# A four-layer graph network in one kernel: softmax and RMS factors laid along the free axis by block transposes instead of by bf16 products

## The chip, the cores and the metric

The kernel runs on one core of a Trainium2 chip. Its time is the device time in microseconds from start to end of one execution. A core has engines that run side by side and meet at semaphores: TensorE (PE, matrix products into PSUM), VectorE (DVE), ScalarE (ACT), GpSimd (POOL) and the queue of SyncE (SP), which issues the transfers between device memory and the on-chip memory SBUF. Each engine works through its own instructions strictly in their order. SBUF and PSUM have 128 partitions; data runs along the free axis inside each of them.

## The reference

There are 32 graphs of 512 nodes, with 256 features each and a 512x512 adjacency matrix. Four layers follow each other, each inside a residual sum and a layer norm:

```python
x = LN(x + attention(x, adj))         # 8 heads of 32, masked by adj
x = LN(x + W2 relu(W1 ((1+eps) x + adj x)))
h = W1 (eps x + adj x) + b1           # 1024 wide
x = LN(x + W2 silu(h * rsqrt(mean(h^2) + 1e-6) * w) + b2)
x = LN(x + softplus(xn W_self + (xn - s_out adj s_in xn) W_neigh))
```

Two factors concern us. The softmax divides each head's output by the sum of its exponentials, one number per node and head. The RMS norm of the third layer multiplies all 1024 hidden values of a node by one number. Everything is computed in float32.

## The kernel before

Hidden values are kept transposed: features on partitions, the 512 nodes along the free axis (oT for the attention's output, gT for the third layer's hidden values). The two factors, however, come out with nodes on partitions, 128 nodes in each of NT = 4 tiles, so they have to be laid along the free axis and repeated over the partitions before they can multiply oT or gT.

For this, `split` (L917) cuts a factor into three bf16 parts whose sum is the float32 number (L924, L931). The parts are transposed on TensorE (pm_t, L941) and copied to SBUF (mT). Products with constant selector matrices then add the three parts and repeat them over partitions: `spread` (pr_r, L970) for the softmax, once per graph for both groups of four heads, and `spread_rms` (pb, L1321) for the RMS. `normalise` (L953) does so after both calls of `attend`: the reciprocals of all 32 sums (L959), the split, pr_r, and the products with oT (L981). oT itself has been copied from PSUM by `evacuate` before. For the RMS, squares of gT are added into ssq by POOL (L554), ssq is block-transposed (L1277) and reduced (L1280), a small product pm (L1288) adds over partitions, two DVE operations pick each node's own number (L1302, L1310), POOL raises it to -0.5 (L572), then come split and pb, and eight DVE operations scale gT (L1333). Silu (L1348) and the w22 product (L998) follow.

In `attend` (L770) the scores sc use row quadrants of TensorE (32 rows each, four heads side by side), and the weighted sums po_att (L900) use column quadrants. Transposing the exponentials takes a DVE block transpose (L858) and a round trip through device memory (L870, L882); graph 0 uses TensorE for it.

The order of all work is not that of the code. Each operation is recorded with its engine, an assumed cost, and what it reads and writes. The class `Order` lays out one graph to find due times, adds a constant per stage (`LEAD`), and gives graph b the key b times `PERIOD` plus that. A list planner then places the operations of all graphs; among those that can start soon the smallest key wins, with penalties for changing TensorE's tiling (`TURN_DUE`) and ACT's table. So several graphs are interleaved, and every engine's queue is fixed before the run. Tiles come from rings of buffers: four PSUM banks for most products, one set of four banks for sc.

Of the kernel before, what the change touches and what calls it, by code (L numbers as in the profile page):

```python
# [9 lines left out]
F32 = mybir.dt.float32  # L10
# [6 lines left out]
P = 128  # L17
# [2 lines left out]
RMS_EPS = 1e-6  # L20
HEADS = 8

PERIOD = 68064
LEAD = {
    "adjT": 136800, "agg1": -11000, "agg2": -29700, "degree": 92400, "diag": 77700,
    "lap": -82300, "ln0": -24200, "ln1": -117600, "ln2": -21700, "ln3": 9700, "load": -153500,
    "move": 42300, "pv": 19300, "pz": 26900, "qk": 7500, "rinv": -106100, "rms": -114100,
    "scores": -6200, "silu": 94000, "softplus": -156100, "v": -89600, "w11": -216800,
    "w12": -58400, "w21": 15900, "w22": -12100, "wo": 64800, "x3T": 800, "xT": 6200,
}  # L30


# [27 lines left out]
class Order:  # L60
# [9 lines left out]
    TABLE, TABLE_DUE = 1300, 9000  # L70

    TURN = {"whole": 93, "row": 290, "col": 150}
    TURN_DUE = 750
    LATE = 0.13
    HASTE = 90

    def __init__(self):
        self.ops = []
# [209 lines left out]
def kernel(  # L288
# [48 lines left out]
    make_identity(nc, ident)  # L337
    ones = const.tile([P, P], F32, name="ones")
    nc.vector.memset(ones, 1.0)
    nhalf = const.tile([P, NT], F32, name="nhalf")  # L340
    nc.vector.memset(nhalf, -0.5)

    ident_b = const.tile([P, P], BF16, name="ident_b")
    nc.vector.tensor_copy(ident_b, ident)

    def selector(n, wide, name):

        of = const.tile([P, n], F32, name=f"{name}_of")
        nc.vector.tensor_reduce(
            of, ident[:, 0 : 3 * n].rearrange("p (r x) -> p x r", r=3), axis=AX.X, op=ALU.add
        )
        sel = const.tile([P, n, wide], BF16, name=name)
        nc.vector.tensor_copy(sel, of.unsqueeze(2).to_broadcast([P, n, wide]))
        return sel

    NX = 2 * NT * HPG
    sel_r = selector(NX, HD, "sel_r")  # L360
    sel_t = selector(NT, P, "sel_t")


    id_as = ident.rearrange("p (a s) -> p a s", a=4)
# [3 lines left out]
    nc.vector.tensor_copy(quad, place.unsqueeze(1).to_broadcast([P, 4, 32]))  # L368
    own = const.tile([P, 4], F32, name="own")
    nc.vector.tensor_reduce(own, id_as, axis=AX.X, op=ALU.add)  # L370
    nc.vector.tensor_single_scalar(own, own, 1.0 / F2, op=ALU.mult)

    order = Order()

# [138 lines left out]
    def graph(b):  # L513
# [10 lines left out]
        def tmp(shape, tag, bufs, name=None, dtype=F32):  # L524
            return Buf(sb, shape, dtype, tag, f"{name or tag}_{b}", bufs)

        def pe(cost, fn, r, w, *hold, turn="whole"):

            op([("PE", cost, fn, {"turn": turn})], r, w, hold)

        def dve(cost, fn, r, w, port=False):
            op([("DVE", cost, fn, {"port": 1} if port else {})], r, w)
# [4 lines left out]
        def pool(cost, fn, r, w):  # L537
            op([("POOL", cost, fn, {})], r, w)
# [4 lines left out]
        def evacuate(dst, src, r, w):  # L543
            either(
                r, w,
                (690, lambda: nc.vector.tensor_copy(dst(), src())),
                (590, lambda: nc.scalar.copy(dst(), src())),
            )
# [19 lines left out]
                port=True,  # L568
            )

        def rsqrt(dst, src, r, w):
            pool(1020, lambda: nc.gpsimd.tensor_tensor(dst(), src(), nhalf, ALU.pow), r, w)  # L572

        def small(name, bufs=2, shape=None):
            return Buf(sb, shape or [P, NT], F32, "s_" + name, f"{name}_{b}", bufs)
# [194 lines left out]
        def attend(g):  # L770
# [5 lines left out]
            for t in range(NT):  # L776
# [113 lines left out]

                if t < NT - 1:
                    continue
                stage[0] = "pv"

                def pv():

# [10 lines left out]

                pe(
                    3500, pv,
                    [(pT, a) for pT in pTs for a in range(4)] + [(v, c) for c in range(NT)],  # L910
                    [(po,)], oT, turn="col",
                )

            stage[0] = "rinv"
            evacuate(lambda: oT[:, g, :], po, [(po,)], [(oT, g)])

        def split(src, n, name):  # L917

            parts = tmp([P, 3, n], "p_" + name, 2, name + "p", dtype=BF16)
            left, left_k = src, []  # L920
            for r in range(3):
                dve(
                    190,
                    lambda r=r, left=left: nc.vector.tensor_copy(parts[:, r, :], left()),  # L924
                    [(left,)], [(parts, r)], port=True,
                )
                if r < 2:
                    rest = small(name + "rest", 2, [P, n])
                    dve(
                        180,  # L930
                        lambda r=r, left=left, rest=rest: nc.vector.tensor_tensor(  # L931
                            rest(), left(), parts[:, r, :], ALU.subtract
                        ),
                        [(left,), (parts, r)], [(rest,)], port=True,
                    )
                    left = rest
            pm_t = Buf(ps, [P, P], BF16, "m", f"pm_t_{b}", 4)
            mT = tmp([P, P], "mT_" + name, 1, dtype=BF16)
            pe(
                65,  # L940
                lambda: nc.tensor.transpose(  # L941
                    pm_t[0 : 3 * n, :], parts().rearrange("p r x -> p (r x)"), ident_b
                ),
                [(parts, r) for r in range(3)], [(pm_t,)], mT,
            )
            either(
                [(pm_t,)], [(mT,)],
                (220, lambda: nc.vector.tensor_copy(mT[0 : 3 * n], pm_t[0 : 3 * n, :])),
                (330, lambda: nc.scalar.copy(mT[0 : 3 * n], pm_t[0 : 3 * n, :])),
            )  # L950
            return mT

        def normalise():  # L953

            stage[0] = "rinv"
            rv = small("rv", 2, [P, NX])
            dve(
                240,
                lambda: nc.vector.reciprocal(rv(), rs().rearrange("p g t j -> p (g t j)")),  # L959
                [(rs, g, t, j) for g in range(2) for t in range(NT) for j in range(HPG)],  # L960
                [(rv,)],
            )
            mT = split(rv, NX, "sums")
            for g in range(2):
                pr_r = bank("pr_r")

                def spread(g=g, pr_r=pr_r):
                    for t in range(NT):
                        x = (g * NT + t) * HPG
                        nc.tensor.matmul(  # L970
                            pr_r[:, t * P : (t + 1) * P],
                            lhsT=sel_r[0 : 3 * NX, x : x + HPG].rearrange("p j e -> p (j e)"),
                            rhs=mT[0 : 3 * NX],
                            start=True,
                            stop=True,
                        )

                pe(240, spread, [(mT,)], [(pr_r,)])
                dve(
                    700,  # L980
                    lambda g=g, pr_r=pr_r: nc.vector.tensor_tensor(  # L981
                        oT[:, g, :], pr_r(), oT[:, g, :], ALU.mult
                    ),
                    [(pr_r,)], [(oT, g)],
                )

        def pair_sum(lhs, lhs_k, w, w_k, nk, y, step):

# [101 lines left out]
        values()  # L1090
        attend(0)
        attend(1)
        normalise()
        stage[0] = "wo"
        pair_sum(oT, lambda k: (oT, k), wo, "wo", DC, y, DC)

# [198 lines left out]
            [(red,)], [(pm,)],  # L1295
        )

        mine = small("mine", 1, [P, NT, 4])
        ms = small("ms")

        def mean_square():
            nc.vector.scalar_tensor_tensor(  # L1302
                out=mine(),
                in0=pm[:, 0 : 4 * NT].rearrange("p (t i) -> p t i", i=4),
                scalar=RMS_EPS * F2,
                in1=own.unsqueeze(1).to_broadcast([P, NT, 4]),
                op0=ALU.add,
                op1=ALU.mult,
            )
            nc.vector.tensor_reduce(ms(), mine(), axis=AX.X, op=ALU.add)  # L1310

        dve(400, mean_square, [(pm,)], [(ms,), (mine,)])
        rr = small("rr")
        rsqrt(rr, ms, [(ms,)], [(rr,)])

        mT = split(rr, NT, "rms")
        pb = bank("pb")

        def spread_rms():
            for t in range(NT):  # L1320
                nc.tensor.matmul(  # L1321
                    pb[:, t * P : (t + 1) * P],
                    lhsT=sel_t[0 : 3 * NT, t],
                    rhs=mT[0 : 3 * NT],
                    start=True,
                    stop=True,
                )

        pe(240, spread_rms, [(mT,)], [(pb,)])
        for m in range(C2):  # L1330
            dve(
                750,
                lambda m=m: nc.vector.scalar_tensor_tensor(  # L1333
                    out=gT[:, m, :],
                    in0=gT[:, m, :],
                    scalar=rw_c[:, m : m + 1],
                    in1=pb(),
                    op0=ALU.mult,
                    op1=ALU.mult,
                ),  # L1340
                [(pb,), ("rw_c",)], [(gT, m)],
            )
        stage[0] = "silu"
        for hf in range(2):
# [256 lines left out]
```

## Time and profile before

| | us |
|---|---|
| median of three runs (lowest, highest) | 3340.49 (3338.41, 3343.99) |
| the profiled execution | 3344.47 |
| its span, first to last instruction | 3342.7 |
| TensorE busy | 3290.4 |
| VectorE busy | 2672.3 |
| ScalarE busy | 1957.1 |
| GpSimd busy | 841.5 |

Busy time is the time in which an engine has at least one instruction running. A float32 product shows as two records, and the records' ends overlap those that follow, so the time a group of products takes is read from its start to the next group's start. The granted TensorE clock was 0.995 of full.

### The profile page before, as it was taken

Reading aid. Unit: us, or ns where it says so; the run is one execution under the profiler, and the core shown is the slowest. Engines: PE = TensorE matmul, PEld = TensorE weight load, DVE = VectorE, ACT = ScalarE, POOL = GpSimd, SP = SyncE. Lnnn points to the kernel's source line nnn. Section 1 sums busy time; section 2 is a strip of 40 time slices with the busy share of each in tenths; the row PEclk is TensorE's granted clock in tenths of the full one; section 3 lists DMA queues with packets and bytes.
Section 4 is the critical chain, followed back from the end, with each engine's and each line's share of the span. In section 5 each row is a group of like instructions: output and inputs, shape, how many; then the busy total and the mean of one; then the engine's idle time right before and its main releaser. Section 6 shows DMA issues by size and latency. Waiting matters only on the chain.

```text
span 3342.7 us, 54840 instructions
## 1 busy us (share of the span) xinstructions
PE 3290.4 (98%) x19624; PEld 1983.0 (59%) x19624; DVE 2672.3 (80%) x6191; ACT 1957.1 (59%) x4056; POOL 841.5 (25%) x611
## 2 busy tenths in 40 slices
PE   8999999999999999999999999999999999999997
PEld 5456665566665566655566655666555666556654
DVE  8878887788887888887888877888878888778855
ACT  6456656556665656665655656566656566656533
POOL 1222222222222222222222222222222222222221
PEclk9999999999999999999999999999999999999999
DMA  6788777777777777887777877877877877877710
GB/s 155 234 230 233 197 207 224 199 226 209 206 216 224 201 218 208 211 225 203 216 215 198 218 224 196 225 206 205 225 215 201 222 205 204 234 196 210 199 38 26
DMA packets 768193, 677.21 MB, mean 203 GB/s; under 512 B 540208, under 2 KB 592304, under 8 KB 736176
## 3 DMA queue, kind: packets, MB, share of 16 engines
q1 hardware_dynamic: 767920, 673.71, 73.7%
q8 instruction: 155, 2.54, 0.3%
q14 instruction: 118, 0.97, 0.1%
HBM read 380.52 MB, written 293.08 MB: 202 GB/s over the span
## 4 chain that ended last, share of the span: by engine, by line
PE 93%; DVE 2%; ACT 2%; DMA 1%; SPq 1%; issue 0%; POOL 0%; POOLq 0%; DVEq 0%; ACTq 0%
PE po L998 23%; PE ph L1177 13%; PE pg L1194 13%; PE sc L784 8%; PE po_att L900 7%; PE pa L1194 7%; PE pq L711 6%; PE pa_l L1485 6%; PE pz L1443 6%; PE pv L752 3%; SPq L595 1%; ACT pq L822 1%; DVE pq L858 0%; PE pr_r L970 0%; DMA xnT<-x3d 0%
## 5 line engine op out<-in xcount | busy, mean ns | idle before, releaser
L822 ACT ACTIVATE pq<-pq,mx 128x512 f32<-128x512 f32 x1024 | 729.1, 713 | 311.6 <-DVE mx L808 292.1
L808 DVE CUSTOM_DVE_ANT_0 pq<-sc,bias 128x512 f32<-128x512 f32 x1024 | 664.7, 683 | 96.5 <-PE sc L784 88.9
L858 DVE STREAM_TRANSPOSE pq<-pq 128x2048 f32<-128x2048 f32 x248 | 569.9, 2298 | 152.6 <-ACT pq L822 151.8
L1194 PE MATMUL pg<-hT,w 128*128 128x512 f32 x1024 | 470.1, 599 | 0.3 <-DVE zy L1454 0.2
L998 PE MATMUL po<-w,gT 128*128 128x256 f32 x2048 | 450.1, 380 | 6.8 <-ACT gT L1348 6.8
L998 PEld LDWEIGHTS po<-w,gT 128*128 128x128 f32 x2048 | 389.8, 191 | 64.4 <-ACT gT L1348 9.6
L554 POOL TENSOR_TENSOR ssq<-ssq,sq 128x512 f32<-128x512 f32 x218 | 277.4, 1272 | 593.2 <-ACT sq L1270 593.2
L1051 POOL TENSOR_TENSOR rstd<-ve,nhalf 128x4 f32<-128x4 f32 (+1 forms) x132 | 134.4, 1018 | 846.4 <-DVE ve L1046 845.4
L1194 PEld LDWEIGHTS pg<-hT,w 128*128 128x128 f32 x1024 | 189.2, 190 | 261.9 <-issue 219.9
L784 PE MATMUL sc<-kT,qT 32*128 32x512 f32 x2048 | 292.9, 641 | 0.0
L900 PEld LDWEIGHTS po_att<-pT,v 128*32 128x32 f32 x8192 | 219.9, 110 | 51.6 <-DVE zy L1454 21.2
L1443 PE MATMUL pz<-wsn,xnT 128*128 128x512 f32 x512 | 242.0, 599 | 3.9 <-DVE s_in L1118 2.2
L900 PE MATMUL po_att<-pT,v 128*32 128x128 f32 x8192 | 237.8, 274 | 3.9 <-DMA pT<-via 3.9
L1177 PE MATMUL ph<-adjT,y_att 128*128 128x512 f32 x512 | 230.5, 603 | 0.0
L998 PE MATMUL po<-w,aT 128*128 128x256 f32 x1024 | 229.5, 382 | 0.0
L1485 PE MATMUL pa_l<-zy,adjT 128*128 128x256 f32 x1024 | 229.2, 382 | 0.0
L1194 PE MATMUL pa<-hT,w 128*128 128x512 f32 x512 | 228.3, 599 | 0.0
L1177 PE MATMUL ph<-adjT,y 128*128 128x512 f32 x512 | 227.5, 596 | 0.0
L998 PEld LDWEIGHTS po<-w,aT 128*128 128x128 f32 x1024 | 192.0, 190 | 48.4 <-issue 22.0
L1485 PEld LDWEIGHTS pa_l<-zy,adjT 128*128 128x128 f32 x1024 | 192.1, 190 | 26.4 <-issue 0.9
L1270 ACT ACTIVATE sq<-gT 128x512 f32<-128x512 f32 x224 | 140.1, 625 | 92.2 <-POOL ssq L554 45.8
L822 ACT ACTIVATION_READ_ACCUMULATOR pq<-pq,mx 128x1 f32 x1024 | 192.2, 188 | 0.0
(166 smaller groups left out, 4687.0 us busy)
## 6 DMA issues: line engine op xcount, KB each, us to landing
via<-pq SPq DMA_DIRECT2D x992, 256.0 KB, 5.1
pT<-via SPq DMA_DIRECT2D x248, 1024.0 KB, 6.7
adj<-in_adj_dram SPq DMA_DIRECT2D x32, 1024.0 KB, 8.6
adjT<-in_adj_dram SPq DMA_DIRECT2D x124, 256.0 KB, 7.1
y_att<-in_x_dram SPq DMA_DIRECT2D x32, 512.0 KB, 4.2
xT<-in_x_dram SPq DMA_DIRECT2D x124, 128.0 KB, 4.0
x3d<-y SPq DMA_DIRECT2D x31, 512.0 KB, 2.9
xnT<-x3d SPq DMA_DIRECT2D x124, 128.0 KB, 7.3
```

Of the source, the lines that this page charges most:

```text
L554: lambda: nc.gpsimd.tensor_tensor(dst(), dst(), src(), ALU.add), {},
L711: nc.tensor.matmul(pq(), lhsT=w[:, c, m * P : (m + 1) * P], rhs=xT[:, c, :], start=(c == 0), stop=(c == DC - 1),)
L784: nc.tensor.matmul(sc[:, j, :], lhsT=qT[hp, g, t * P : (t + 1) * P], rhs=kTs[g][hp, :], start=True, stop=True,)
L808: lambda t=t, j=j, sc=sc, row=row: nc.vector.tensor_tensor_reduce(out=row(), in0=sc[:, j, :].rearrange("p (a n) -> p a n", a=4), in1=bias[ ...
L822: lambda t=t, j=j, row=row: nc.scalar.activation(row(), row(), AF.Exp, bias=mx[:, t, j : j + 1], scale=-1.0, accum_out=rs[:, g, t, j : j + 1],
L858: lambda pq=pq: nc.vector.transpose(pq().rearrange("p a j c s -> p (a j c s)"), pq().rearrange("p a j c s -> p (a j c s)"),),
L900: nc.tensor.matmul(po[j * HD : (j + 1) * HD, t * P : (t + 1) * P], lhsT=v[:, c, h * HD : (h + 1) * HD], rhs=pTs[t][:, :, j, c, :], start=( ...
L998: nc.tensor.matmul(po[:, i * D : (i + 1) * D], lhsT=lhs[:, k, t * P : (t + 1) * P], rhs=w[:, k, :], start=(i == 0 and k == 0), stop=(i == ...
L1177: nc.tensor.matmul(ph(), lhsT=xin[:, m, c * P : (c + 1) * P], rhs=adjT[:, m, :], start=(m == 0), stop=(m == NT - 1),)
L1194: nc.tensor.matmul(pa(), lhsT=w[:, c, m * P : (m + 1) * P], rhs=hT[:, c, :], start=(c == 0), stop=(c == DC - 1),)
L1443: nc.tensor.matmul(pz(), lhsT=xnT[:, c, t * P : (t + 1) * P], rhs=wsn[:, c, :], start=(c == 0), stop=(c == DC - 1),)
L1485: nc.tensor.matmul(pa[:, i * D : (i + 1) * D], lhsT=adjT[:, m, t * P : (t + 1) * P], rhs=zy[:, m, D : 2 * D], start=(m == 0), stop=(m == N ...
```

## The change

The selectors, `split`, `normalise`, pm_t, pr_r and pb are gone. A new helper `along` does the laying out: a DVE transpose in blocks of 32x32 whose source is a column repeated 32 times, so that one instruction gives a 128x512 tile.

For the softmax, each call of `attend` now takes the reciprocals of its own 16 sums, multiplies them with the constant own (a mask that keeps, on each partition, one of four quarters) into parts, and a small product pf, per head, in column quadrants with 16 columns, spreads them; `along` makes fac from pf. po_att is recorded as waiting for pf. Its result is multiplied with fac straight from PSUM, with no copy before.

For the RMS, the two picking operations become one on all 16 columns, POOL's power takes 16 columns, and `along` makes the tile that scales gT. The scale 1/F2 moves from own into that operation.

The planner's parameters are other ones too, so the whole order changes. The number of products on TensorE falls from 10116 to 9924. Per graph: two pm_t, eight pr_r and four pb go, eight pf come.

```diff
-PERIOD = 68064
+PERIOD = 73093
 LEAD = {
...
-    TURN_DUE = 750
-    LATE = 0.13
-    HASTE = 90
+    TURN_DUE = 2500
+    LATE = 0.00
+    HASTE = -18005
...
-    nhalf = const.tile([P, NT], F32, name="nhalf")
+    nhalf = const.tile([P, 4 * NT], F32, name="nhalf")
...
+        def along(dst, src, r, w):
+            dve(
+                700,
+                lambda: nc.vector.transpose(
+                    dst().rearrange("p (x r) -> p x r", r=32),
+                    src().unsqueeze(2).to_broadcast([P, 4 * NT, 32]),
+                ),
+                r, w,
+            )
...
+                    160, lambda: nc.vector.reciprocal(rv(), rs[:, g]),
...
+                    lambda: nc.vector.tensor_tensor(
+                        parts().rearrange("p j t i -> p (j t) i"),
+                        rv().rearrange("p t j -> p j t").unsqueeze(3).to_broadcast([P, HPG, NT, 4]),
+                        own.unsqueeze(1).to_broadcast([P, HPG * NT, 4]),
+                        ALU.mult,
+                    ),
...
+                def quadrants():
+                    for j in range(HPG):
+                        nc.tensor.matmul(
+                            pf[j * HD : (j + 1) * HD, 0 : 4 * NT],
+                            lhsT=quad[:, 0, :],
+                            rhs=parts[:, j].rearrange("p t i -> p (t i)"),
+                            start=True,
+                            stop=True,
+                        )
+                pe(
+                    120, quadrants,
+                    [(parts,)] + [(pT, a) for pT in pTs for a in range(4)]
+                    + [(v, c) for c in range(NT)],
+                    [(pf,)], fac, turn="col",
+                )
+                along(fac, lambda: pf[:, 0 : 4 * NT], [(pf,)], [(fac,)])
...
-            evacuate(lambda: oT[:, g, :], po, [(po,)], [(oT, g)])
...
+                lambda: nc.vector.tensor_tensor(oT[:, g, :], po(), fac(), ALU.mult),
+                [(po,), (fac,)], [(oT, g)],
...
-        normalise()
...
+        ms, rr = (small(n, 1, [P, 4 * NT]) for n in ("ms", "rr"))
+        dve(
+            170,
+            lambda: nc.vector.tensor_scalar(
+                ms(), pm[:, 0 : 4 * NT], scalar1=1.0 / F2, scalar2=RMS_EPS,
+                op0=ALU.mult, op1=ALU.add,
+            ),
+            [(pm,)], [(ms,)],
+        )
+        rsqrt(rr, ms, [(ms,)], [(rr,)], 4 * NT)
+        along(ssq, rr, [(rr,)], [(ssq,)])
```

## The prediction

> **What bounds the kernel now.** I read the page first: busy times and slices.
>
> ```profile
> PE 3290.4 (98%) x19624; PEld 1983.0 (59%) x19624; DVE 2672.3 (80%) x6191; ACT 1957.1 (59%) x4056; POOL 841.5 (25%) x611
> ...
> PE   8999999999999999999999999999999999999997
> ```
>
> TensorE is busy for 98% of the span; only the first and last slices fall short. The windows say where the other 2% lies (columns: window, length, busy us of PE, weight loads, DVE, ACT, POOL, then clock and DMA).
>
> ```profile
> 1500.00:1600.00 100.00, 100.00 (x602) 59.73 (x602) 81.12 (x187) 59.45 (x127) 26.40 (x19) 1.00 0.75 214
> ...
> 0.00:300.00 300.00, 279.77 (x1941) 169.45 (x1942) 245.85 (x578) 174.12 (x397) 60.30 (x48) 0.99 0.76 209
> 3100.00:3342.00 242.00, 210.97 (x1094) 136.02 (x1092) 149.36 (x366) 98.70 (x156) 49.69 (x40) 0.95 0.34 86
> ```
>
> Idle at the head are 20 us, at the tail 31; of the 51 to 52 in all (3342.7 - 3290.4) nothing is left for the middle. So a graph costs what its TensorE instructions take, and the next view is TensorE's timeline over one period (start, length, tile). Two equal softmax products (po_att) start at 1513.73 and 1615.38 us: a period of 101.65 us, 32 of them in the span.
>
> ```profile
> 1544.17 1.14 PE L784 MATMUL sc<-kT,qT 32*128 32x512 f32 x8
> 1545.24 0.26 PE L941 MATMUL pm_t<-ident_b,sumsp 128*96 128x128 bf16 x1
> 1545.34 1.94 PE L711 MATMUL pq<-xT,wk 128*128 128x512 f32 x4
> 1547.11 0.61 PE L970 MATMUL pr_r<-mT_sums,sel_r 96*128 96x128 bf16 x8
> 1547.56 7.08 PE L1177 MATMUL ph<-adjT,y 128*128 128x512 f32 x16
> ...
> 1577.71 1.14 PE L784 MATMUL sc<-kT,qT 32*128 32x512 f32 x8
> 1578.78 3.70 PE L900 MATMUL po_att<-pT,v 128*32 128x128 f32 x128
> 1582.41 0.40 PE L1288 MATMUL pm<-red,quad 128*128 128x16 f32 x2
> 1582.65 7.15 PE L1485 MATMUL pa_l<-zy,adjT 128*128 128x256 f32 x32
> 1589.64 1.03 PE L752 MATMUL pv<-wv,xT 128*128 128x256 f32 x4
> 1590.60 0.22 PE L941 MATMUL pm_t<-ident_b,rmsp 128*12 128x128 bf16 x1
> 1590.75 1.99 PE L752 MATMUL pv<-wv,xT 128*128 128x256 f32 x8
> 1592.68 0.39 PE L1321 MATMUL pb<-mT_rms,sel_t 12*128 12x128 bf16 x4
> 1593.00 1.13 PE L752 MATMUL pv<-wv,xT 128*128 128x256 f32 x4
> ```
>
> Ends overlap, so I cost everything from start to next start.
>
> **TensorE: what goes.** Per graph: the two bf16 transposes pm_t, 1545.24 to 1545.34 and 1590.60 to 1590.75, 0.25 us; pr_r, 1547.11 to 1547.56, 0.45; pb, 1592.68 to 1593.00, 0.32. Sum 1.02. They also cut other work: pv takes 0.96 + 1.93 + 1.06 = 3.95 us in three pieces, where its 16 records of 256 columns at 0.215 us (pg and pz, unbroken, pass four records of 512 columns in 1.72 us) plus the 0.14 to 0.2 us that a run loses ahead of sc make 3.6; pq loses 0.05. I take 0.35 + 0.05, so **1.4 us removed**.
>
> **TensorE: what comes.** pf, twice a graph: four fp32 products 128x32 by 16 columns, two records each, eight in all, in the four column quadrants. The trace has none. Nearest row: po_att, same shape of array, 128 records in 3.63 us, 28 ns each, so 8 records = 0.23. Lower end: hidden among the turns, 0.1. Upper end: if each of the eight weight loads is exposed at its 110 ns (the mean load of po_att), 0.9. I take 0.25. It also makes a turn of the array. In the changed program's order 60 of the 64 pf stand apart from po_att: once between pz and sc, once between sc and pq, with po_att after pq. That is one turn more per pf. A turn is priced by sc: 1.07 us for two rounds of 512 columns that need 0.86 at that rate, 0.21 over, and po_att's 3.63 against 3.43 says the same. **Added: 2 x (0.25 + 0.21) = 0.92; I take 1.0 us**; range 0.6 to 2.2.
>
> Here the Trainium skill speaks against the change. "TensorEngine Tiling (Array Packing)", Key Properties: a change of tiling mode drains TensorE. Its Instruction Overhead section: every matmul carries about 60 cycles, so that few columns cost as much as 60. By the rule pf's 16 columns are worth nearly four times their width and both its borders are drains; an estimate from that page with two full drains per pf, at sc's 0.21, is 2 x (0.23 + 0.42) = 1.30 us, which would nearly cancel the saving. The rows show 0.21 per turn, and the order shows that pf mostly exchanges one border for another, so I keep 1.0.
>
> Net per graph -1.4 + 1.0 = -0.4 us, times 32 = **-13 us** (bounds -0.8 x 32 = -26 and +0.8 x 32 = +26).
>
> **DVE, ACT, POOL: off the bound, if the order holds.** DVE loses the splits (ten operations of 126 to 206 ns, 1.64 us), one 351 ns reciprocal and two 170 ns operations; it gains two reciprocals (no more than 0.35 each), two products with own (0.2 each), ms 0.17, and three block transposes. Nearest row for these: the ssq transpose of the same 128x512, 707 ns; a stride-0 source or PSUM could make it 1.4. Net +1.05 us a graph, hidden by the 19% that DVE is idle. ACT loses oT's copy twice (576) and two mT copies (about 250): 1.65 less. Without DVE's idle time the 1.05 would be 34 us.
>
> POOL's power runs on 16 columns instead of 4. The row shows that columns count:
>
> ```profile
> L1051 POOL TENSOR_TENSOR rstd<-ve,nhalf 128x4 f32<-128x4 f32 x124 | 128.7, 1038 | 794.5 <-DVE ve L1046 794.5
> L1051 POOL TENSOR_TENSOR rstd<-ve,nhalf 128x2 f32<-128x2 f32 x8 | 5.7, 711 | 51.9 <-DVE ve L1046 50.9 <-DVE nmr L1058 1.0
> ```
>
> (1038 - 711)/2 = 163 ns a column, so 16 columns = 1038 + 12 x 163 = 3.0 us; lower end 1.0 if the rest is fixed cost. I take 3.0.
>
> **The wait that matters.** The RMS chain (pm, ms, power, transpose, gT scaling, silu) releases the w22 products. Before, w22 starts 18.0 us after pm (1582.41 to 1600.41). In the new order only pa_l (7.0), wo (3.5) and sc with its turn (1.25) stand between: 11.7 us. The chain from pm, with the DVE queue in its new order: pm and its signal 0.6; ms 0.2; oT 0.7; the pq transpose, 2.24, which covers the power (started 0.25 after ms, done at about 4.0, against 3.8 for the transpose); the new transpose 0.7; zy 0.5; four gT scalings at 0.66 each (eight take from 1593.11 to 1598.38) 2.6; silu 1.9. Sum about 9.7. Slack 2 us, so no stall; before, the first silu half ended at 1599.06, a slack of 1.4. Behind the transpose that waits for POOL stand zy, the eight scalings and the y_att additions of wo on DVE; for these wait w22, the next graph's agg1, and sc's bank. I followed those too: sc's bank is free about 2 us early, agg1's input about 1.4.
>
> po_att now waits for pf, which waits for the softmax sums; these end before the block transpose and two DMAs (5.1 and 6.7 us by the issues) that po_att needs anyway: nothing. wo waits for oT after po_att: about 0.9 us of slack. At the tail, the last w22 has only four pa_l products (1.75 us) ahead of it where it had 10.9: about 7 us lost, against 4.8 + 1.7 + 0.9 us of idle in the old tail that the new order fills. The head loses some 6 us likewise at the first w22 and saves the 3.3 us wait for pT and other small ones. Ramp together 0, plus or minus 8.
>
> **Sum.** The profiled execution took 3344.47 us: span 3342.7 and 1.8 around it. Minus 13: 3331.5. The median before is 3340.49, 4 less than that execution, so I predict **3327.5 us**.
>
> **Rivals.**
> - *Stall at w22.* If the chain exceeds 11.7 us, TensorE waits in every graph; it decides at 2 us over my sum. A power above 5 us, or DVE arriving late at pm, does it. For: POOL's price grows with columns, and the cover fell from 18 to 11.7. Against: the power lies under the pq transpose. One us past the point: 31 - 13 = 3358; two: 3389. Slower. Chance 0.24, with other waits from the reshuffled order.
> - *Turns eat it.* pf costs 0.7 with its turn, by the rule above: 2 x 0.7 = 1.4, nothing is left: 3340. For: the rule; against: the 0.21 rows. Chance 0.16.
> - *Cheaper than thought.* pf at 0.1 with turns 0.2: net -0.8: 3315. Chance 0.12.
> - *The forecast*, 3318 to 3333: chance 0.48.
>
> **How the numbers follow.** 0.2% of 3340 is 6.7 us, about what a measurement of this kernel can tell from none. Faster: forecast and cheap case, 0.60; same 0.15; slower 0.25. The range for 8 in 10 runs from the cheap case with a good ramp, 3308, to a stall of one us past its point, 3360; the likeliest case alone has 3318 to 3333.
>
> **What would show it.** Right: TensorE at 100.00 in middle windows; a po_att-to-po_att period near 101.25; pf and its neighbours about 0.5 us longer; the 16-column power near 3.0 us; transposes near 0.7; DVE busy 2706, ACT 1904. Wrong: waits of po (w22) for gT, or of ph, repeated some 30 times; pf's group at 0.7 us or more.

## The result, and the profile after

| | before | after |
|---|---|---|
| median of 12 runs each, alternating, us | 3342.59 | 3344.51 |
| profiled execution, us | 3344.47 | 3344.42 |
| its span, us | 3342.7 | 3342.6 |
| TensorE busy, us | 3290.4 | 3263.1 |
| TensorE idle within the span, us | 52.3 | 79.5 |

The ratio of the times is 1.0005, interval 0.9997 to 1.0013: no change that can be measured. The forecast was 3327.5 us, 17 us too low, and most of its chance lay on "faster". Yet TensorE's own work fell by 27.3 us, twice what was forecast. Its idle time grew by 27.2 us, and this cancels it.

The page of the kernel after, its row of busy times:

```profile
PE 3263.1 (98%) x19688; PEld 1972.2 (59%) x19688; DVE 2735.2 (82%) x6097; ACT 1896.6 (57%) x3886; POOL 925.2 (28%) x610
```

The windows of the kernel after (columns as before) tell where the idle time lies:

```profile
0.00:300.00 300.00, 279.89 (x1840) 168.79 (x1841) 240.05 (x556) 172.16 (x394) 64.68 (x48) 0.98 0.73 202
300.00:3100.00 2800.00, 2772.89 (x16750) 1668.21 (x16749) 2339.58 (x5183) 1624.33 (x3332) 806.73 (x524) 1.00 0.78 213
3100.00:3342.00 242.00, 210.33 (x1101) 135.16 (x1099) 155.56 (x361) 100.13 (x162) 53.80 (x38) 0.94 0.34 87
```

Head and tail are as before: 20.1 us idle against 20.2, and 31.7 against 31.0. The middle, where before had 0.3 us (2799.67 busy of 2800), now has 27.1. The clock there is 1.00 in both, so it isn't the reason. The view of waits names the place (columns: who waited and for what; us in total, times, longest):

```profile
PE pq L704 <- DVE y L979: 27.1, 27, 1.0
PE po L965 <- ACT gT L1294: 16.9, 2, 11.5
```

The first line is the whole of it: 27 waits of 1.0 us, about one in every graph. A product pq, which makes kT for the attention of a later graph, waits for a DVE addition at L979. The two have no data in common. L979 is the addition that takes w22's result out of PSUM (y <- po, y), and the product needs the PSUM bank that it empties. The second line is w22 waiting for the RMS chain at the first and last graph only; nothing of the kind repeats.

TensorE's timeline of the kernel after, over the stretch that the prediction showed of before and then around the wait. From sc at 1498.14 to the same sc at 1600.00 a period is 101.86 us; it was 101.65.

```profile
1498.14 1.14 PE L777 MATMUL sc<-kT,qT 32*128 32x512 f32 x8
...
1574.43 0.26 PE L911 MATMUL pf<-parts,quad 128*32 128x16 f32 x8
1574.62 1.14 PE L777 MATMUL sc<-kT,qT 32*128 32x512 f32 x8
1575.69 3.70 PE L932 MATMUL po_att<-pT,v 128*32 128x128 f32 x128
1579.32 0.40 PE L1254 MATMUL pm<-red,quad 128*128 128x16 f32 x2
...
1600.00 1.14 PE L777 MATMUL sc<-kT,qT 32*128 32x512 f32 x8
1601.08 5.45 PE L965 MATMUL po<-w,gT 128*128 128x256 f32 x24
1606.36 3.62 PE L745 MATMUL pv<-wv,xT 128*128 128x256 f32 x16
...
1617.41 1.98 PE L704 MATMUL pq<-xT,wk 128*128 128x512 f32 x4 [1.02 <-DVE y L979]
1619.24 1.88 PE L1143 MATMUL ph<-adjT,y_att 128*128 128x512 f32 x4
```

pf takes 0.19 us to the next start, and pv in one piece 3.45 (1606.36 to 1609.81) where it took 3.95. The last-but-one line has the loss: TensorE was free from 1616.39 on.

w22's products had ended by 1606.36, ten microseconds earlier. Why does the bank come free so late? DVE's timeline of the kernel after:

```profile
1610.60 0.36 DVE L1025 SCALAR_TENSOR_TENSOR nmr<-mv,rstd 128x4 f32<-128x4 f32 x1
...
1612.14 0.16 DVE L1095 TENSOR_TENSOR s_out<-s_out,s_out 128x4 f32<-128x4 f32 x1
1612.22 2.30 DVE L851 STREAM_TRANSPOSE pq<-pq 128x2048 f32<-128x2048 f32 x1
1614.45 0.13 DVE L1105 TENSOR_SCALAR ns_out<-s_out 128x4 f32<-128x4 f32 x1
1614.48 2.30 DVE L851 STREAM_TRANSPOSE pq<-pq 128x2048 f32<-128x2048 f32 x1
1616.71 1.25 DVE L979 TENSOR_TENSOR y<-po,y 128x512 f32<-128x512 f32 x2
```

The same stretch on POOL:

```profile
1608.52 2.42 POOL L1117 TENSOR_TENSOR y<-y_att,b_r 128x1024 f32<-128x1024 f32 x1 [0.61 <-ACT y_att L1044]
1610.87 1.23 POOL L553 TENSOR_TENSOR s_out<-s_out,nhalf 128x4 f32<-128x4 f32 x1
```

DVE has no gap here, but in its order the two additions stand behind L1095 and two block transposes of 2.3 us each. L1095 waits for POOL's power on s_out, which stands behind POOL's long addition L1117 and ends at 1612.10. So the bank is released about 1.0 us after TensorE wants it.

### The profile page after: what moved, and what is told of

It is laid out like the page before. It is cut to its first block, busy times and chain, and to the rows that moved or that the text cites. A ratio compares the mean times of both kernels' runs of the same rounds, so it can differ in the third digit from the quotient of the medians.

```text
span 3342.6 us, 54684 instructions
## 1 busy us (share of the span) xinstructions
PE 3263.1 (98%) x19688; PEld 1972.2 (59%) x19688; DVE 2735.2 (82%) x6097; ACT 1896.6 (57%) x3886; POOL 925.2 (28%) x610
## 4 chain that ended last, share of the span: by engine, by line
PE 80%; DVE 5%; ACT 3%; POOL 3%; issue 2%; DMA 0%; SPq 0%; POOLq 0%; DVEq 0%; ACTq 0%
PE po L965 20%; PE pg L1160 12%; PE ph L1143 8%; PE pz L1389 6%; PE sc L777 6%; PE pa_l L1431 6%; PE pq L704 6%; PE po_att L932 6%; PE pa L1160 6%; DVE pq L851 4%; POOL y L1117 2%; ACT adjT L632 2%; POOL s_out L553 1%; ACT y_att L1044 1%; DVE y L979 1%
## 5 line engine op out<-in xcount | busy, mean ns | idle before, releaser
L801 DVE CUSTOM_DVE_ANT_0 pq<-sc,bias 128x512 f32<-128x512 f32 x1024 | 657.0, 683 | 99.1 <-PE sc L777 58.0
L965 PE MATMUL po<-w,gT 128*128 128x256 f32 x2048 | 463.4, 385 | 16.9 <-ACT gT L1294 16.9
L1160 PE MATMUL pg<-hT,w 128*128 128x512 f32 x1024 | 447.8, 595 | 0.0
L1215 DVE TENSOR_SCALAR gT<-pg,b_c 128x512 f32<-128x512 f32 x161 | 120.8, 750 | 170.3 <-PE pg L1160 170.0
L1431 PE MATMUL pa_l<-zy,adjT 128*128 128x256 f32 x1024 | 243.1, 382 | 0.0
L1143 PE MATMUL ph<-adjT,y_att 128*128 128x512 f32 x512 | 239.3, 602 | 2.1 <-issue 1.7
L1294 ACT ACTIVATE gT<-gT 128x2048 f32<-128x2048 f32 x64 | 122.4, 1914 | 188.7 <-DVE gT L1279 188.7
L1389 PE MATMUL pz<-wsn,xnT 128*128 128x512 f32 x512 | 226.8, 595 | 0.1
```

The source lines that it names most:

```text
L801: lambda t=t, j=j, sc=sc, row=row: nc.vector.tensor_tensor_reduce(out=row(), in0=sc[:, j, :].rearrange("p (a n) -> p a n", a=4), in1=bias[ ...
L965: nc.tensor.matmul(po[:, i * D : (i + 1) * D], lhsT=lhs[:, k, t * P : (t + 1) * P], rhs=w[:, k, :], start=(i == 0 and k == 0), stop=(i == ...
L1143: nc.tensor.matmul(ph(), lhsT=xin[:, m, c * P : (c + 1) * P], rhs=adjT[:, m, :], start=(m == 0), stop=(m == NT - 1),)
L1160: nc.tensor.matmul(pa(), lhsT=w[:, c, m * P : (m + 1) * P], rhs=hT[:, c, :], start=(c == 0), stop=(c == DC - 1),)
L1389: nc.tensor.matmul(pz(), lhsT=xnT[:, c, t * P : (t + 1) * P], rhs=wsn[:, c, :], start=(c == 0), stop=(c == DC - 1),)
L1431: nc.tensor.matmul(pa[:, i * D : (i + 1) * D], lhsT=adjT[:, m, t * P : (t + 1) * P], rhs=zy[:, m, D : 2 * D], start=(m == 0), stop=(m == N ...
```

## The experiments

All ratios are against the kernel before, run alternately on the same chip. It stood at 3342.57 us beside e1, e6, e4 and e2, at 3343.89 beside e5, e7, e3 and e8, at 3344.04 beside e9 and at 3342.66 beside e10.

### The wait taken away in two ways

In the first kernel (e1) the w22 additions are moved ahead of the two transposes in DVE's queue, and of L1095, which stands with them. Only the finished order is changed:

```diff
-        out = self.run(self.ops, lambda o: keys[o.n])
+        out = sums_first(self.run(self.ops, lambda o: keys[o.n]))
...
+def sums_first(out):
+    for i in range(len(out)):
+        o = out[i]
+        if o.stage != "w22" or o.way[0] != "DVE":
+            continue
+        to = i
+        for k in range(i - 1, -1, -1):
+            q = out[k]
+            if q.n in o.preds:
+                break
+            if q.way[0] != "DVE":
+                continue
+            if q.stage not in ("move", "degree"):
+                break
+            to = k
+        out.insert(to, out.pop(i))
+    return out
```

> The changed kernel; in each graph the two VectorE additions that empty the w22 products' PSUM banks are put ahead of the two 2.3 us transposes of exponentials that stood before them. Nothing else moves. Theory (a PSUM bank given back too late makes the kT product wait 1.0 us in each of 27 graphs): the additions come 4.5 us earlier, the wait goes, period 100.86 instead of 101.86 us, about 3342.6 - 27 = 3316 us, ratio 0.992. Rival (VectorE simply has too much work in this stretch): the wait turns up at another product with about the same size, 3340 to 3346 us.

In the second (e6), TensorE's order is changed and DVE's left alone: the product that waits moves behind the agg1 product (ph) that followed it (j and k are the next and the last operation on TensorE).

```diff
-        out = self.run(self.ops, lambda o: keys[o.n])
+        out = keys_later(self.run(self.ops, lambda o: keys[o.n]))
...
+def keys_later(out):
...
+        if o.stage == "qk" and engine(i) == "PE" and o.b > 0:
...
+            if (
+                j < len(out) and out[j].stage == "agg1" and out[k].stage == "agg1"
+                and not any(o.n in out[x].preds for x in range(i + 1, j + 1))
+            ):
+                out.insert(j, out.pop(i))
```

> The changed kernel with VectorE's order as it is; on TensorE the kT product that waits is put behind the next agg1 product, so that it is wanted 1.72 us later. Theory (the bank is 1.0 us late for it): no wait, 3316 us, ratio 0.992, the same as with the additions moved. Rival (too much VectorE work): TensorE still loses 1 us per graph somewhere, 3340 to 3346 us.

Measured: e1 3319.30 us, ratio 0.9928 (0.9915 to 0.9940); e6 3311.12 us, 0.9902 (0.9886 to 0.9917). The windows of e6:

```profile
300.00:3100.00 2800.00, 2800.00 (x17028) 1696.81 (x17027) 2375.72 (x5248) 1638.08 (x3370) 814.73 (x530) 1.00 0.78 215
```

TensorE's timeline of e6 around the moved product:

```profile
1496.64 5.42 PE L1143 MATMUL ph<-adjT,y_att 128*128 128x512 f32 x12
1501.90 3.60 PE L704 MATMUL pq<-xT,wk 128*128 128x512 f32 x8
```

The middle is full again, and pq follows ph with no wait. A period is 100.61 us (sc at 1483.95, the next at 1584.56): 1.04 less than before. This times 32 is 33 us, and the ratio gives 0.0098 x 3342.57 = 32.8. So 1.04 us per graph is what the changed operations save on TensorE. The lost time follows as well: 101.86 - 100.61 = 1.25 us per graph with a wait, of which the records show 1.0 as idle; 27 x 1.25 = 34 us, against 33.4 between the medians of after and e6. The other 0.25 stands in the rows beside the wait. The eight records of ph ahead of it last 3.70 us to their modelled end; without a wait the next product would start after 3.54 (e6's twelve take 5.26 to the next start, less four at 0.43). The four of pq behind it take 1.83 to the next start, where four in an unbroken stream take 1.72.

e1 gains 8 us less. Its view of waits has the first line gone and a new one:

```profile
PE sc L777 <- ACT qT L730: 6.8, 12, 1.1
```

Both kernels change only an order, one on DVE and one on TensorE, and in both the 27 waits are gone. This is the cause of the missing gain. e6 is the cleaner proof: in its program the product keeps its bank, while in e1's the banks are dealt out anew. Both kernels are also faster than before and after.

### Is it the 16-column power, or the new DVE operations?

POOL's power on 16 columns took 2912 ns in after. In this kernel (e4) it takes 4 of the 16, and the block transpose repeats those four:

```diff
-                lambda: nc.gpsimd.tensor_tensor(dst(), src(), nhalf[:, 0:n], ALU.pow), r, w,
+                lambda: nc.gpsimd.tensor_tensor(dst()[:, 0:NT], src()[:, 0:NT], nhalf[:, 0:NT], ALU.pow), r, w,
...
-        along(ssq, rr, [(rr,)], [(ssq,)])
+        few = lambda: rr[:, 0:NT].unsqueeze(1).to_broadcast([P, NT, NT])
+        along(ssq, few, [(rr,)], [(ssq,)])
```

> The changed kernel, same order on every engine; the power runs on 4 of the 16 columns and the transpose after it repeats these four (the RMS factors are so wrong for part of the nodes; the work is otherwise the same). Power 2.91 us becomes 1.03. Theory: the power lies under a transpose and the wait comes from elsewhere, so the time stays, 3340 to 3346 us, the ramp perhaps 2 to 4 us shorter. Rival (the longer power makes VectorE late and so causes the wait): 1.0 us less per graph, 3316 us.

3339.86 us, ratio 0.9991 (0.9983 to 1.0000). The power took 1017 ns, and the view of waits of e4 is all but that of after:

```profile
PE pq L704 <- DVE y L979: 27.0, 27, 1.0
```

Only the wait of the last w22 shrank, from 11.5 to 9.6 us: there the chain through the power does set the end, and 1.9 us is the power's own saving. In the middle it is covered, as forecast.

The next kernel (e9) moves the new reciprocal and the product with own behind the w22 additions on DVE, some 0.3 us of work (o is the second addition, near the 14 DVE operations ahead of it):

```diff
-        out = self.run(self.ops, lambda o: keys[o.n])
+        out = factors_last(self.run(self.ops, lambda o: keys[o.n]))
...
+def factors_last(out):
...
+        for q in [q for q in near if q.stage == "rinv" and q.way[1] in (160, 190)]:
+            k = out.index(q)
+            if not any(q.n in x.preds for x in out[k + 1 : i + 1] if x.stage != "rinv"):
+                out.remove(q)
+                out.insert(out.index(o) + 1 + (q.way[1] == 190), q)
```

> The changed kernel; on VectorE the reciprocal and the product parts, the only new operations between the scores of sc and the late additions, are put behind these additions. In the profile the two take about 0.3 us of that queue. Theory (order: sixteen us of old work stand ahead of the additions, the new operations are a small part): the wait of the kT product shrinks from 1.0 to 0.7 us, 27 x 0.3 = 8 us less, 3334 to 3337 us. Rival (the new operations are the cause): the wait goes, 3316 us.

3342.21 us, ratio 0.9997 (0.9988 to 1.0006): my expectation of a gain was wrong. The view of waits of e9:

```profile
PE pq L704 <- DVE y L979: 26.1, 27, 1.0
```

The timeline of e9 on DVE tells why:

```profile
1610.21 0.51 DVE L1025 SCALAR_TENSOR_TENSOR nmr<-mv,rstd 128x4 f32<-128x4 f32 x1
...
1611.88 0.16 DVE L1095 TENSOR_TENSOR s_out<-s_out,s_out 128x4 f32<-128x4 f32 x1
```

The moved operations leave DVE early enough, but the time goes elsewhere: nmr, 0.13 us at 1606.11, lasts 0.51 here, and DVE meets POOL's power at L1095 just as late (the whole stretch lies 0.22 us earlier than in after, and L1095 only 0.26). So the new operations aren't the cause. What holds the additions back is what e1 puts them ahead of: L1095, which waits for POOL's pair of operations, and the two transposes, 4.5 us by the records. No run moved POOL's pair by itself.

### More of the same wait

Here (e10) one extra DVE operation stands ahead of the first w22 addition and puts it 0.30 us later.

```diff
-    order = Order()
+    order = Order(); dull = const.tile([P, 512], F32, name="dull"); nc.vector.memset(dull, 0.0)
...
-                    lambda tp=tp, po=po: nc.vector.tensor_tensor(
+                    lambda tp=tp, po=po: (w_k == "w22" and tp == 0 and nc.vector.tensor_scalar_add(dull, dull, 1.0)) and None or nc.vector.tensor_tensor(
```

> The changed kernel with one more VectorE operation, a constant added to a 128x512 tile nobody reads, directly ahead of each graph's first w22 addition and behind the two transposes. Theory: the PSUM bank comes back later by the operation's own time d and TensorE's wait grows one for one, from 1.0 to 1.0 + d us in 27 graphs; with d about 0.5 us some 13 us more, 3356 us. Rival (the wait has another cause, and VectorE has slack): no change, 3342 us.

3346.78 us, ratio 1.0013 (1.0006 to 1.0019). Waits and timeline of TensorE in e10:

```profile
PE pq L704 <- DVE y L979: 29.7, 22, 1.7
```

```profile
1516.08 1.88 PE L704 MATMUL pq<-xT,wk 128*128 128x512 f32 x4
...
1618.18 1.98 PE L704 MATMUL pq<-xT,wk 128*128 128x512 f32 x4 [1.34 <-DVE y L979]
```

And DVE in e10:

```profile
1516.84 1.28 DVE L979 TENSOR_TENSOR y<-po,y 128x512 f32<-128x512 f32 x2
...
1617.14 0.39 DVE L979 TENSOR_SCALAR dull<-dull 128x512 f32<-128x512 f32 x1
1617.44 1.28 DVE L979 TENSOR_TENSOR y<-po,y 128x512 f32<-128x512 f32 x2
```

A wait is 1.35 us on average (29.7 / 22) where it was 1.0: the delay of 0.30 passes on about one for one. But there are five fewer, which is why the time rose by little. In five graphs (5, 13, 16, 22 and 30) the program gives the product another bank, one that ACT empties. Its wait in the program is on ACT there, and at 1516.08 it runs although the addition starts only at 1516.84. This is the plainest evidence that the bank alone ties the two together.

### The planner's parameters

Two kernels separate the operations from the parameters: the new operations with the old parameters (e2; all of `LEAD` too), and the reverse (e3).

```diff
-PERIOD = 73093
+PERIOD = 68064
...
-    TURN_DUE = 2500
-    LATE = 0.00
-    HASTE = -18005
+    TURN_DUE = 750
+    LATE = 0.13
+    HASTE = 90
```

> The changed operations with the planner parameters of the kernel before. Theory: the operations alone save 0.8 us of TensorE per graph; the parameters only decide which waits come. If this order has no wait, 3316 us; each wait of 1 us per graph adds 27 to 30. Rival (the operations themselves bring the wait): about 3342 us or more.

```diff
-PERIOD = 68064
+PERIOD = 73093
...
-    TURN_DUE = 750
-    LATE = 0.13
-    HASTE = 90
+    TURN_DUE = 2500
+    LATE = 0.00
+    HASTE = -18005
```

> The operations of the kernel before with the planner parameters of the changed one. Theory (operations and parameters belong together; an order planned with parameters found for other operations brings waits): slower than 3342 us, by 1 us per graph and wait, 3360 us and more. Rival (the new parameters make a worse order by themselves and are the cost that ate the gain): 3370 us, the 27 us of the changed kernel's waits on top of the time before. Rival (parameters are neutral): 3342 us.

e2: 3595.63 us, ratio 1.0754 (1.0732 to 1.0776). e3: 3502.07 us, 1.0470 (1.0455 to 1.0486). Each is far slower than I thought. TensorE idles for 254.7 and 166.7 us. That isn't all of it: its busy time grew too, in e2 from after's 3263.1 to 3333.1 us at a granted clock of 0.972 instead of 0.994, and in e3 from before's 3290.4 to 3329.5 at 0.989 instead of 0.995. The clock would account for the 70 us in e2 (3263.1 x 0.994 / 0.972 = 3337) and for some 20 of the 39 in e3; why less was granted, no run tests. The costliest wait of e2:

```profile
PE sc L777 <- DVE mx L801: 60.8, 30, 5.0
```

and of e3:

```profile
PE pa_l L1485 <- DVE gT L1333: 74.3, 27, 2.8
```

Each of the two sets of parameters fits the operations it was made for and not the other, so the two halves can't be valued apart. With the wrong set, a kernel of the same work loses 4.7% (e3 against before) or 7.5% (e2 against after), by waits and by a lower clock; after's set fits its operations but for one wait.

### Prices of the removed and the added products

In before, with pr_r and pb issued twice (e8; the second place, in `spread_rms`, has the same edit):

```diff
-                    for t in range(NT):
+                    for t in [*range(NT), *range(NT)]:
```

> The kernel before with the eight pr_r and the four pb products of a graph issued twice, the same result. The prediction priced them at 0.45 and 0.32 us per graph: 0.77 x 32 = 25 us more than before, 3367 us. If part of that price is only the change from float32 to bf16 and back, which doubling does not repeat, 12 to 20 us more.

3361.64 us, ratio 1.0050 (1.0033 to 1.0067), span 20.7 us longer. TensorE in e8:

```profile
1555.44 1.06 PE L970 MATMUL pr_r<-mT_sums,sel_r 96*128 96x128 bf16 x16
1556.34 7.09 PE L1177 MATMUL ph<-adjT,y 128*128 128x512 f32 x16
```

pr_r takes 0.90 us, twice its 0.45, and pb 0.55 (1601.46 to 1602.01), 0.23 more than its 0.32. Together 0.68 x 32 = 22 us in the rows; the times give 17 (11 to 22). The prediction's price for both was 25. So most of it is confirmed; about 0.1 us of pb's price comes once, however often pb is issued.

On the other side, e6 with each pf issued five times (e7):

```diff
-                    for j in range(HPG):
+                    for j in [j for _ in range(5) for j in range(HPG)]:
```

> The kernel of e6 with the four pf products issued five times in a row, the same result each time: four more sets of eight records, 64 times. By the recorded prediction's body of 0.25 us per set: 4 x 64 x 0.25 = 64 us more than e6, 3375 us. By the 0.08 us that one pf takes in the profile of e2 where it stands beside po_att: 4 x 64 x 0.08 = 20 us more, 3331 us.

3328.19 us, ratio 0.9950 (0.9935 to 0.9965), span 15.9 us longer than e6. TensorE in e7:

```profile
1530.77 0.54 PE L911 MATMUL pf<-parts,quad 128*32 128x16 f32 x40
1531.24 1.98 PE L704 MATMUL pq<-xT,wq 128*128 128x512 f32 x4
```

The group takes 0.47 us against 0.19 in e6, so four more sets of eight records cost 0.28: 0.07 us a set, 9 ns a record.

Last (e5), e6 with each pf put directly ahead of its po_att, which has the same column quadrants, and with its block transpose directly ahead of oT's multiplication (o is pf's group, lay the transpose, mul the multiplication):

```diff
-        out = keys_later(self.run(self.ops, lambda o: keys[o.n]))
+        out = beside(self.run(self.ops, lambda o: keys[o.n]))
...
+def beside(out):
+    out = keys_later(out)
...
+        out.remove(o)
+        out.insert(out.index(po), o)
+        out.remove(lay)
+        out.insert(out.index(mul), lay)
+    return out
```

> The kernel of e6 (kT product one place later); in addition each pf is put directly before its po_att on TensorE, both in column quadrants, and its block transpose directly before the multiplication of oT on VectorE. One turn of the array less per pf. The recorded prediction's price (0.21 us a turn) gives 2 x 0.21 x 32 = 13 us less than e6: 3298 us. Rival (a turn costs little where the products around it are long, as pf's 0.19 us in the profile suggests): 0 to 6 us less, 3305 to 3311 us. If the later block transpose makes oT late for the wo product, some 0.5 us a graph more, 3327 us.

3303.44 us, ratio 0.9878 (0.9863 to 0.9892): 1.2% faster than before, and the fastest of all. TensorE in e5:

```profile
1556.45 1.14 PE L777 MATMUL sc<-kT,qT 32*128 32x512 f32 x8
1557.52 0.26 PE L911 MATMUL pf<-parts,quad 128*32 128x16 f32 x8
1557.61 3.68 PE L932 MATMUL po_att<-pT,v 128*32 128x128 f32 x128
```

Beside po_att, pf takes 0.09 us. The period falls from e6's 100.61 to 100.36 us (1481.54 to 1581.90), 0.25 for two pf, and the ratios give 0.0024 x 3343 = 8 us, the same times 32. One pf now saves a turn, so 0.12 us is the price of one, with all counted in that changes for the products beside it.

## Why the prediction was wrong

**The bound: right.** TensorE sets the time in both kernels, and each microsecond of its wait or work shows in the total.

**What goes, 1.4 us: right in its main terms.** pm_t, pr_r and pb are gone with their 1.02 (e8 supports it for the two larger). pv won 0.50 where I took 0.35; pg and pz together won another 0.20 that I did not count. w22 pays 0.21 back, since a score product now stands in it, and wo and pa_l 0.08. Net about 1.43.

**What comes, 1.0 us: mis-sized, 0.45 measured.** A pf takes 0.18 to 0.19 us where it stands, and pq between pf and po_att another 0.09, so two pf cost 0.45. I had priced the body at 0.25 from po_att's 28 ns a record of 128 columns; it is 0.07 to 0.08, since a record of 16 columns passes in 9 ns (e7). I had priced a turn at 0.21 from what sc takes over its columns; e5 against e6 gives 0.12. The estimate from "TensorEngine Tiling (Array Packing)" (Key Properties and Instruction Overhead), 1.30 us, is further off, and its body of 0.23 wasn't the page's: that was the price of all 128 columns. The page puts few columns at the price of 60, by po_att's rate an estimate of 28 x 60 / 128 = 13 ns a record. The 9 measured lie below that and above the 3.5 that 16 columns would take by their width: few columns cost more than their width, as the page says, though less than it says.

The net saving was therefore about 1.0 us a graph and not 0.4: 33 us, as e6 shows. The case "cheaper than thought", with 0.8, came nearest to it.

**The waits: the step that failed.** The prediction looked for the wait in the RMS chain and then said: "I followed those too: sc's bank is free about 2 us early, agg1's input about 1.4." I had followed those who wait for data behind the RMS transpose, and one bank, that of the scores. I had not followed the four product banks, nor what stands ahead of the w22 additions on DVE: POOL's pair L1117 and L553, L1095, and two transposes. In the new order a kT product comes 26 us after w22 starts (1591.17 to 1617.41) and takes a bank that these additions empty. That a product wants such a bank soon is not new: in the program of before the first of them goes to the second half of ph, some 22 us after w22's start (1600.41 to about 1622.5, half way through ph's products at 1619.02). New is that DVE comes late. The same additions in before:

```profile
1612.69 0.69 DVE L1012 TENSOR_TENSOR y<-po,y 128x512 f32<-128x512 f32 x1
...
1615.03 0.66 DVE L1012 TENSOR_TENSOR y<-po,y 128x512 f32<-128x512 f32 x1
```

There the first starts 12.3 us after w22 and leaves some 9 us to spare; in after it starts 25.5 us after (1616.71), behind the two transposes. This costs 1.25 us in 27 graphs, 34 us, and takes all of the gain. The rival *stall at w22* allowed for "other waits from the reshuffled order" but gave neither place nor price; its own mechanism did not happen. *Turns eat it* gave nearly the right time, 3340, for a reason that e5 and e7 refute. That the time lies between 3308 and 3360 is luck as well: a saving taken too small and a wait overlooked cancelled.

**The RMS chain: right.** These groups of the kernel after have the durations that were forecast (3.0 for the power, 0.7 for the transposes):

```profile
L553 POOL TENSOR_TENSOR rr<-ms,nhalf 128x16 f32<-128x16 f32 x32 | 93.2, 2912 | 205.8 <-DVE ms L1267 205.8
L560 DVE STREAM_TRANSPOSE fac<-pf 128x512 f32<-128x512 f32 x64 | 43.6, 681 | 0.0
L560 DVE STREAM_TRANSPOSE ssq<-rr 128x512 f32<-128x512 f32 x32 | 21.8, 680 | 7.8 <-POOL rr L553 7.8
```

From pm at 1579.32 the first silu half ends at 1589.25, 9.9 us (forecast 9.7), and w22 starts at 1591.17, 11.85 after pm (forecast 11.7). A slack of 1.9 us, forecast 2.

**The rest.** The ramp came to 0 as forecast: the head is the same and the tail 0.7 us longer, though the last w22 waits 11.5 us where about 7 were forecast. ACT is busy for 1896.6 us (forecast 1904). DVE is busy for 2735 (forecast 2706): the new order puts 30 more evictions of gT on it, 161 against 131 at 750 ns, 22 us that the forecast left out. The remark that DVE's time is hidden holds for its amount and not for its order: DVE idles for 18% of the span, and yet holds a bank for 1 us too long in almost every graph.

## What to carry to other kernels

When a change reshuffles an order in which one engine is always busy, follow every buffer that this engine writes to the instruction that empties it, and ask what stands ahead of that instruction on its own engine; data dependences alone don't show such waits. If a saving on the bounding engine doesn't show in the time, compare its busy and its idle time stage by stage, and look for a short wait that repeats once in each iteration. Parameters that shape an order belong to the operations they were made for: judge a change of operations with an order that fits it, and then mend its last wait by hand, as e6 and e5 do.

## What was not expected of the hardware

- Small products cost little: eight fp32 records of 16 columns in column quadrants add 0.07 us, and a turn of the array 0.12 us.
- The power on POOL costs by the column: in the same place 1017 ns for four (e4) and 2912 for sixteen (after), so (2912 - 1017) / 12 = 158 ns each on average.
- The 128x512 block transpose takes 680 ns from a repeated column of SBUF and 681 from one of PSUM; with an ordinary source it was 707.
- A DVE operation of four columns (nmr) lasts 0.13 us at 1606.33, but 0.36 at 1610.60 in after and 0.51 at 1610.21 in e9, and ends within 0.03 us of POOL's addition of 2.4 us both times (1610.96 against 1610.94, 1610.72 against 1610.69). Its operand rstd isn't what was late: in after that power had ended by 1607.91. Why the two end together, no run tests.
